# A 16-image approximate-matmul convolution block: ranking lookups, first-map scatters, second-layer centring and next-image loads at other steps

## The chip, the cores and the metric

The kernel runs on one core of one Trainium2 chip. A core has five engines that run their own instruction queues: TensorE (PE in the profile; its weight loads are PEld), VectorE (DVE), ScalarE (ACT), GpSimd (POOL) and SyncE (SP, whose queue issues most DMAs). 16 DMA engines serve all queues. The metric is the device time of one execution in microseconds (us); lower is better.

## The reference

A block of 16 images (256 channels, 28 x 28), all in fp32. Each image is group-normalized (32 groups), then goes through two layers in which a 3x3 convolution is replaced by a lookup: per channel, the 9-element patch is compared with 16 centroids, the softmax of the negated distances weighs the centroids, and the weighted centroid goes through the weights.

```python
def amm_conv3x3(x, centroids, w_sub):          # C channels, k=16 codes, s=9
    p = patches3x3(x)                          # b, n, C, s
    d = sum(p*p) - 2*einsum('bncs,cks->bnck', p, centroids) + sum(centroids*centroids)
    attn = softmax(-d)                         # over the 16 codes
    lut = einsum('cks,cso->cko', centroids, w_sub)
    return einsum('bnck,cko->bno', attn, lut)

out = relu(bn1(amm_conv3x3(gn(x), centroids1, wsub1)))
out = bn2(amm_conv3x3(out, centroids2, wsub2))
out = out * sigmoid(relu(mean(out) @ w1 + b1) @ w2 + b2)
result = x + relu(out + gn(x))
```

## The kernel before

**Tiling and steps.** The work is cut into blocks: layer (2) x image (16) x half of the channels (`hh`) x half of the rows (`t`), 128 blocks in all, four to an image. A block takes two steps, so an image is 8 steps; layer 0 of image `b` starts its blocks at step `8b`, layer 1 follows from step 128. In each step PE runs, in this order: 32 records of logits (`lg`, L388), 64 records of either denominators (`nb`, L452, in even steps) or numerators (`na`, L438, in odd steps), 32 more logits, and then a product of up to 18 records (`acc`, L522). The four blocks of an image are combined with seven products instead of eight (a Strassen scheme), for which POOL forms differences of the quotients (`mix`, L529 and L531). Products of steps 8n+6 and 8n+7 have 14 and 4 records, so these two steps are short.

**What one block needs.** SP loads 3x3 patches from a padded image in DRAM (`home1`, `home2`) into `pt` (L373, L376), six DMAs for each step. PE makes logits, ACT the exponentials (L399), PE `nb`, ACT and DVE the reciprocal (L462, L466, L480), DVE spreads it (L495), PE makes `na`, and DVE (L514) or ACT and POOL (L508, L503) scale it to the quotients `qp` and `qo`.

**Side work.** Between the blocks of layer 0 the kernel prepares layer 1. Channels are sorted by a score after image 0 (the *ranking*): `rank_row` loads the scores of all channels (L643, L644), `rank_make` compares them on POOL (L651 to L654), `rank_sum` counts on DVE (L659), `rank_look` gathers a table row for each channel (L666, two indirect DMAs on POOL), and `rank_cols` copies its columns (L675). From image 1 on, `to_home2` scatters the first layer's output to DRAM in that order (L594, four indirect DMAs for each image). Image 0 was finished before the order was known, so its two maps are kept in `d_h0`, read back by `h0_load` (L691) and scattered by `h0_put` (L594 again, with the source `st`). Later steps build layer 1's codes in the same staging tile `st`: `prep_wd2` and `prep_wd3` add the squared norms (L285, L290, L291), `prep_wd4` centres them over the 16 codes (`center_mean`: a DVE sum L295 and a scaling L296, then two POOL subtractions L297 and L743), `prep_keep` writes them out (L746); `prep_cw0` and `prep_cwa` (L751, L761) and `prep_cwb` (L769 to L771) build the other two. `load_x` (L162) reads the next image into the single tile `xt`; `gn_stats` and `gn_apply` read it.

**What sets the order.** Nothing is reordered by a scheduler here. Each piece of work is entered with `at(step, place, function, ...)`, and all entries are emitted in the order of `(step, place)`; each engine runs its instructions in that order, waiting on semaphores where data or buffers are not ready. Within a step, logits stand at 0.1 and 1.1, `nb` and `na` at 1.0, patch loads at 1.5, products at 2.0.

```python
def at(cl, sub, f, *a, **kw):
    jobs.setdefault((cl, sub), []).append((f, a, kw))
...
at(g + 5, 2.5, mix, us[0], mm, us[1], us[0])
at(g + 7, 1.35 if mm in (4, 0) else 1.25, mix, us[1], mm, us[2], us[1])
```

Of the kernel before, what the change touches and what calls it, by code (L numbers as in the profile page):

```python
# [12 lines left out]
ALU = mybir.AluOpType  # L13
AX = mybir.AxisListType
# [3 lines left out]
P = 128  # L18
# [7 lines left out]
K = 16  # L26
# [49 lines left out]
def kernel(  # L76
# [20 lines left out]
    nc = tc.nc  # L97
# [180 lines left out]
    cst = const.tile([P, 64], F32, name="cst")  # L278
# [9 lines left out]
    def center_add(wf, c0, w, sq, step=None):  # L288
        ps = small_bank("sqp", step)
        nc.tensor.matmul(ps[:, :w], lhsT=nhalf_sb, rhs=sq[:, :w], start=True, stop=True)  # L290
        nc.vector.tensor_add(wf[:, c0 : c0 + w], wf[:, c0 : c0 + w], ps[:, :w])  # L291

    def center_mean(wf, n, eng=None):
        g = wf.rearrange("p (g k) -> p g k", k=K)
        nc.vector.tensor_reduce(cst[:, : n // K], g, axis=AX.X, op=ALU.add)  # L295
        nc.vector.tensor_scalar_mul(cst[:, : n // K], cst[:, : n // K], 1.0 / K)  # L296
        (eng or nc.vector).tensor_sub(g, g, cst[:, : n // K].unsqueeze(2).to_broadcast([P, n // K, K]))  # L297

    def center(wf, n):
        for c0 in range(0, n, 256):  # L300
            center_add(wf, c0, 256, center_sq(wf, c0, 256))
        center_mean(wf, n)
# [381 lines left out]
    pw = {}  # L684
# [51 lines left out]
    def prep_wd3(part, step):  # L736
        center_add(pw["st"][:, 512:1536], 384 * part, min(384, 1024 - 384 * part), pw["sq"], step)

    def prep_wd4():
        st = pw["st"]  # L740
        center_mean(st[:, 512:1536], 1024, nc.gpsimd)
        f = st[:, 512:1536].rearrange("p (g n) -> p g n", n=32)
        nc.gpsimd.tensor_sub(f, f, kbias.unsqueeze(1).to_broadcast([P, 32, 32]))  # L743

# [151 lines left out]
    def at(cl, sub, f, *a, **kw):  # L896
        jobs.setdefault((cl, sub), []).append((f, a, kw))
# [10 lines left out]
    for j, u in enumerate(blocks):  # L908
        gi, g = 8 * (j // 4), 2 * j
# [11 lines left out]
    for j, u in enumerate(blocks):  # L921
        g = 2 * j
# [35 lines left out]
    for l in range(2):  # L958
        for b in range(B):
            n = l * B + b  # L960
            g = 8 * n
            us = blocks[4 * n : 4 * n + 4]
            for c, w, r, ks in PRODUCTS:
                at(g + c, 2.0, product, (n, c), us[r], w, ks, step=g + c)
            for mm in (1, 2, 3, 4, 0):
                at(g + 5, 2.5, mix, us[0], mm, us[1], us[0])
                at(g + 7, 1.35 if mm in (4, 0) else 1.25, mix, us[1], mm, us[2], us[1])
                at(g + 8, 1.37 if mm == 1 else 1.4, mix, us[0], mm, us[2], us[0])
                at(g + 10, 1.4, mix, us[0], mm, us[0], us[3])
            c11, c12, c21, c22 = (0, 0), (0, 1), (1, 0), (1, 1)  # L970
            at(g + 6, 0.0, acc_copy, l, b, c11, (n, 5))
            at(g + 6, 2.02, acc_copy, l, b, None, (n, 6))
            at(g + 8, 0.0, acc_add, l, b, None, (n, 7))
            at(g + 8, 2.02, acc_add, l, b, c21, (n, 8), c11)
            at(g + 10, 0.0, acc_add, l, b, c22, (n, 9), c11, pop=False)
            at(g + 10, 0.01, acc_add, l, b, c21, (n, 9))
            at(g + 10, 0.05, reg_add, l, b, c12, c22, None)
            at(g + 10, 0.06, reg_add, l, b, c22, c21, None)
            at(g + 10, 2.02, acc_add, l, b, c12, (n, 10))
            at(g + 12, 0.0, acc_add, l, b, c11, (n, 11))  # L980
            at(g + 12, 2.02, acc_add, l, b, c21, (n, 12), op=ALU.subtract)
            if l == 0 or b == B - 1:
                at(g + 11, 1.9, norm_out, l, b, *c12)
                at(g + 11, 1.91, norm_out, l, b, *c22)
                at(g + 12, 1.9 if l else 0.05, norm_out, l, b, *c11)
                at(g + 13, 1.06, norm_out, l, b, *c21)
            else:
                for o in range(NB):
                    at(g + 12 + o, 1.9, norm_both, b, o)
            if l == 0:  # L990
                for o in range(2):
                    if b == 0:
                        at(g + 13, 1.9, rank_score, o)
                        at(g + 13, 1.91, rank_keep, o)
                        at(g + 12 + 2 * o, 0.65 if o else 1.93, h0_keep, o)
                    else:
                        for r in range(2):
                            at(g + 12 + o + (o and r), (0.06, 1.97)[r] if o == 0 else (1.805, 2.9)[r], to_home2, b, o, r)
                if b + 1 < B:
                    at(*((g - 2, 2.6) if b else (1, 1.65)), load_x, b + 1)  # L1000
                    for q in range(NB):
                        at(*((g, 0.3) if b else (3, 1.9)), gn_stats, b + 1, q)
                    at(*((g + 1, 2.1) if b else (4, 1.02)), gn_mean, b + 1, step=g + 1 if b else 4)
                    at(*((g + 3, 2.1) if b else (4, 1.11)), gn_var, b + 1, step=g + 3 if b else 4)
                    for q in range(NB):
                        at(g + 4, 1.9, gn_apply, b + 1, q)
                        at(g + 4, 1.92, to_home1, b + 1, q)
            else:
                last = b == B - 1
                at(*((g + 11, 0.6) if last else (g + 13, 2.6)), load_x, b, last)  # L1010
                at(g + 14 - last, 2.1, se_hidden, b, g + 14 - last)
                at(*((g + 14, 1.05, se_gate, b, g + 14) if last else (g + 17, 2.1, se_gate, b, g + 17)))
                at(*((g + 14, 1.05) if last else (g + 18, 0.3)), se_recip, b)
                for q in range(NB):
                    at(*((g + 12, 0.4) if last else (g + 19, 1.9)), finish_norm, b, q)
                    if not last:
                        at(g + 18, 1.9, finish_gate, b, q)
                        at(g + 20, 0.05, finish_sum, b, q)
                        at(g + 20, 1.9, finish_relu, b, q)
                        at(g + 20, 2.2, finish_add, b, q)  # L1020
                        at(g + 20, 2.25, store, b, q)
                    else:
                        at(g + 14, 1.92, finish_fast, b, q)
                        at(g + 14, 1.92, store, b, q)
                if b == B - 1:
                    at(g + 11, 1.9, flags)
                    at(g + 12, 2.9, flag_sum)
# [13 lines left out]
    for o in range(2):  # L1041
        at(14, 2.95, rank_make, o)
        at(16, 0.2, rank_sum, o)
        at(18, 2.15, rank_look, o)
    for o in range(2):
        at(19 + o, 2.7, rank_cols, o)
        at(24 + 2 * o, 0.6 + 2 * o, h0_load, o)
        for r in range(2):
            at(25 + 2 * o + r, 0.2 if r else 1.9, h0_put, o, r)
        at(32 + 2 * o, 2.6, codes_load, o)  # L1050
        for i in range(2):
            at(33 + 2 * o, 1.9, codes_put, o, i)
        for part in range(2):
            c = 40 + 8 * o + 2 * part
            at(c, 2.6, sub_load, o, part)
            at(c + 1, 1.9, sub_put, o, part)
# [3 lines left out]
    for part in range(3):  # L1060
        c = (68, 70, 76)[part]
        at(c, 1.95, prep_wd2, part)
        at(c + 1, 2.1, prep_wd3, part, c + 1)
    at(78, 1.9, prep_wd4)
    at(78, 2.7, prep_keep, d_wd[1])
    at(80, 2.6, prep_cw0)
    at(82, 1.9, prep_cwa)
    for part in range(4):
        at((83, 84, 91, 92)[part], (2.3, 1.5, 2.3, 1.5)[part], prep_cwb, part)
    at(92, 2.7, prep_keep, d_cwb)  # L1070
    at(92, 2.3, load_se)
    for n in range(3):
# [3 lines left out]
    g = 8 * B  # L1076
# [195 lines left out]
```

## Time and profile before

| What | us |
|---|---|
| Median of 3 runs | 2642.16 |
| Lowest and highest of them | 2637.82 and 2643.82 |
| The profiled execution: its time | 2646.4 |
| The profiled execution: its span, first to last instruction | 2644.9 |
| Mean granted PE clock in it | 0.996 |

| Engine | Busy us | Share of the span |
|---|---|---|
| PE | 2595.2 | 98% |
| POOL | 1905.0 | 72% |
| DVE | 1758.2 | 66% |
| ACT | 1357.2 | 51% |

The page of the profile gives busy time for each engine and the chain of work that ended last, followed back from the last instruction. A timeline gives for one engine the start, the length, the line, the operation, what it writes and reads, and in brackets the idle time ahead of it with what ended it. Matmuls overlap and their ends are modelled, so a stall of PE often shows as a longer group rather than as idle time: 32 logits take 0.94 us in most steps, 64 `na` or `nb` records 2.92 us. A quiet image of layer 0 (steps 98 to 106) takes 80.03 us from its first `nb` to the next image's, and each image of layer 1 takes 80.32.

### The profile page before, as it was taken

How to read it: one execution, taken by the hardware profiler on the slowest of the kernel's cores; microseconds unless marked ns; L12 is line 12 of the kernel's file. 1: busy time of each engine (PE TensorE's matmuls, PEld its weight loads, DVE VectorE, ACT ScalarE, POOL GpSimd, SP SyncE). 2: the span in 40 equal slices, each digit the busy share in tenths (PEclk: the TensorE clock that was granted, in tenths of full speed). 3: DMA queues.
4: the chain of work that ended last, by engine and by line, in shares of the span. 5: the costliest groups of instructions: out<-in, count | busy, mean ns of one | idle time of the engine just before them, and what ended most of it. 6: DMA issues, size and time to landing. Idle time of an engine off the chain costs nothing.

```text
span 2644.9 us, 85672 instructions
## 1 busy us (share of the span) xinstructions
PE 2595.2 (98%) x36984; PEld 1266.4 (48%) x36984; DVE 1758.2 (66%) x3760; ACT 1357.2 (51%) x1874; POOL 1905.0 (72%) x1330
## 2 busy tenths in 40 slices
PE   5999999999999999999999999999999999999997
PEld 2444444444444445444444444444444444444444
DVE  4776566665566655665666776767677667767665
ACT  4444444454444544444454555556555655555653
POOL 3866667765667666676567878778878787777786
PEclk9999999999999999999999999999999999999999
DMA  8656656666556666665664445544454544445441
GB/s 201 163 158 173 175 163 167 186 181 168 143 133 157 172 170 165 173 167 148 159 176 109 105 120 128 125 117 107 111 128 121 121 116 115 114 118 127 114 118 48
DMA packets 217735, 374.37 MB, mean 142 GB/s; under 512 B 30136, under 2 KB 187624, under 8 KB 217352
## 3 DMA queue, kind: packets, MB, share of 16 engines
q1 hardware_dynamic: 210408, 334.87, 50.8%
q0 software_dynamic: 6944, 33.95, 3.6%
q8 instruction: 295, 4.83, 0.8%
q14 instruction: 88, 0.72, 0.1%
HBM read 288.93 MB, written 79.80 MB: 139 GB/s over the span
## 4 chain that ended last, share of the span: by engine, by line
PE 96%; DVE 2%; POOL 1%; DMA 0%; issue 0%; ACT 0%; DVEq 0%; POOLq 0%
PE acc L522 51%; PE lg L388 17%; PE nb L452 14%; PE na L438 13%; POOL qp L531 0%; DVE rb L495 0%; DMA pt<-home 0%; DVE r L480 0%; PE sqp L290 0%; DVE qp L514 0%; PE sep L820 0%; POOL qp L503 0%; PE sep L809 0%; DMA xt<-in_x 0%; PE gnp L341 0%
## 5 line engine op out<-in xcount | busy, mean ns | idle before, releaser
L399 ACT ACTIVATE e<-lg 128x784 f32<-128x784 f32 x960 | 738.5, 820 | 661.7 <-PE lg L388 657.2
L531 POOL TENSOR_TENSOR qp<-qp,qp 128x784 f32<-128x784 f32 x512 | 943.5, 1867 | 156.1 <-DVE qp L514 155.6
L522 PE MATMUL acc<-qp,w_S 128*128 128x392 f32 x2048 | 734.5, 501 | 2.5 <-POOL qp L531 1.1
L495 DVE STREAM_SHUFFLE rb<-r 128x392 f32<-128x392 f32 x1024 | 551.0, 604 | 0.0
L522 PE MATMUL acc<-qp,w_A 128*128 128x392 f32 x1536 | 546.5, 499 | 0.0
L522 PEld LDWEIGHTS acc<-qp,w_S 128*128 128x128 f32 x2048 | 376.1, 190 | 346.5 <-issue 51.6
L388 PE MATMUL lg<-pt,wd 32*32 32x392 f32 x16384 | 492.8, 504 | 18.5 <-DMA pt<-home 5.2
L522 PEld LDWEIGHTS acc<-qp,w_A 128*128 128x128 f32 x1536 | 284.1, 190 | 247.6 <-DVE qp L514 39.6
L466 DVE SCALAR_TENSOR_TENSOR r<-nb,kst,r 128x392 f32<-128x392 f32 x128 | 79.9, 624 | 461.2 <-ACT r L462 449.0
L438 PE MATMUL na<-e,cwa 64*32 64x392 f32 x8192 | 376.5, 492 | 1.2 <-ACT e L399 0.7
L452 PE MATMUL nb<-e,cwb 64*32 64x392 f32 x8192 | 376.8, 494 | 0.1
L514 DVE TENSOR_TENSOR qp<-na,rb 128x784 f32<-128x784 f32 x352 | 333.6, 972 | 60.2 <-PE na L438 46.4
L503 POOL TENSOR_TENSOR qo<-qo,rb 128x392 f32<-128x392 f32 x128 | 131.2, 1025 | 315.6 <-DVE rb L491 314.8
L480 DVE RECIPROCAL r<-r 128x392 f32<-128x392 f32 x128 | 333.2, 2603 | 4.4
L503 POOL TENSOR_TENSOR qp<-qp,rb 128x784 f32<-128x784 f32 x160 | 297.0, 1866 | 3.4 <-issue 0.3
L452 PEld LDWEIGHTS nb<-e,cwb 64*32 64x32 f32 x8192 | 191.3, 107 | 178.4 <-issue 28.6
L438 PEld LDWEIGHTS na<-e,cwa 64*32 64x32 f32 x8192 | 182.7, 106 | 186.0 <-issue 75.8
L388 PEld LDWEIGHTS lg<-pt,wd 32*32 32x32 f32 x16384 | 122.7, 103 | 299.5 <-issue 249.2
L462 ACT ACTIVATE r<-nb,kst 128x392 f32<-128x392 f32 x128 | 86.7, 677 | 169.0 <-PE nb L452 169.0
L423 POOL TENSOR_TENSOR z<-z,mx 128x1568 f32<-128x1568 f32 x32 | 91.8, 2869 | 94.7 <-DVE mx L417 94.7
L508 ACT COPY qp<-na 128x784 f32<-128x784 f32 x160 | 129.9, 812 | 24.6 <-PE na L438 23.0
L529 POOL TENSOR_TENSOR qo<-qo,qo 128x392 f32<-128x392 f32 x128 | 131.2, 1025 | 0.0
(151 smaller groups left out, 1658.1 us busy)
## 6 DMA issues: line engine op xcount, KB each, us to landing
pt<-home SPq DMA_DIRECT2D x768, 209.0 KB
pt<-home SPq DMA_DIRECT2D x756, 104.5 KB
home<-xpad SPq DMA_DIRECT2D x31, 899.0 KB
xt<-in_x SPq DMA_DIRECT2D x30, 784.0 KB
out_dram<-y SPq DMA_DIRECT2D x32, 392.0 KB
d_wS<-st SPq DMA_DIRECT2D x12, 192.0 KB
w_S<-d_wS SPq DMA_DIRECT2D x4, 576.0 KB
w_A<-in_ws SPq DMA_DIRECT2D x3, 576.0 KB
```

What stands on the lines that cost most here:

```text
L388: nc.tensor.matmul(bk[32 * c : 32 * c + 32, :N].rearrange("p (r w) -> p r w", w=W), lhsT=wts["wd", u["hh"]][32 * i : 32 * i + 32, mm, c, : ...
L399: nc.scalar.activation(eg[:, 2 * i : 2 * i + 2, :], bk[:, :, :N], AF.Exp, scale=2.0)
L438: nc.tensor.matmul(bs[32 * i : 32 * i + 32, r, :N], lhsT=wts["cwa", u["hh"]][64 * r : 64 * r + 64, mm, i, :], rhs=es[64 * r : 64 * r + 64, ...
L452: nc.tensor.matmul(bs[32 * i : 32 * i + 32, r, :N], lhsT=wts["cwb", u["hh"]][64 * r : 64 * r + 64, mm, i, :], rhs=es[64 * r : 64 * r + 64, ...
L480: nc.vector.reciprocal(u["r"], u["r"])
L495: nc.vector.stream_shuffle(rb[:, r, :], u["r"], mask_of(2 * mm + r))
L503: nc.gpsimd.tensor_tensor(q, q, u.pop(("rb", mm)), ALU.mult)
L508: nc.scalar.copy(pair(u, mm), u.pop(("na", mm))[:, :, :N])
L514: nc.vector.tensor_mul(pair(u, mm), u.pop(("na", mm))[:, :, :N], rb)
L522: nc.tensor.matmul(accs[key][:, :N], lhsT=wl[w][:, k, :], rhs=us["q", k], start=first and n == 0, stop=last and n == len(ks) - 1,)
L529: nc.gpsimd.tensor_tensor(out_u["q", 8], in0["q", 8], in1["q", 8], ALU.subtract)
L531: nc.gpsimd.tensor_tensor(pair(out_u, mm), pair(in0, mm), pair(in1, mm), ALU.subtract)
```

## The change

Only the places in the order change, and `center_mean` is cut in two functions so that its DVE part can stand at a place of its own. `load_x` of the images after the second moves one step ahead. The computation is the same.

```diff
-    def center_mean(wf, n, eng=None):
+    def center_sum(wf, n):
+        nc.vector.tensor_reduce(cst[:, : n // K], wf.rearrange("p (g k) -> p g k", k=K), axis=AX.X, op=ALU.add)
+        nc.vector.tensor_scalar_mul(cst[:, : n // K], cst[:, : n // K], 1.0 / K)
+
+    def center_mean(wf, n):
+        center_sum(wf, n)
         g = wf.rearrange("p (g k) -> p g k", k=K)
...
+        nc.vector.tensor_sub(g, g, cst[:, : n // K].unsqueeze(2).to_broadcast([P, n // K, K]))
...
+    def prep_wd_sum():
+        center_sum(pw["st"][:, 512:1536], 1024)
+
     def prep_wd4():
         st = pw["st"]
-        center_mean(st[:, 512:1536], 1024, nc.gpsimd)
+        g = st[:, 512:1536].rearrange("p (g k) -> p g k", k=K)
+        nc.gpsimd.tensor_sub(g, g, cst.unsqueeze(2).to_broadcast([P, 64, K]))
         f = st[:, 512:1536].rearrange("p (g n) -> p g n", n=32)
         nc.gpsimd.tensor_sub(f, f, kbias.unsqueeze(1).to_broadcast([P, 32, 32]))
...
-                    at(*((g - 2, 2.6) if b else (1, 1.65)), load_x, b + 1)
+                    at(*((g - 3, 2.6) if b else (1, 1.65)), load_x, b + 1)
...
-        at(18, 2.15, rank_look, o)
+        at(17, 1.9, rank_look, o)
     for o in range(2):
-        at(19 + o, 2.7, rank_cols, o)
-        at(24 + 2 * o, 0.6 + 2 * o, h0_load, o)
+        at(18, 2.7, rank_cols, o)
+        at(24 + 4 * o, 0.1 if o else 0.6, h0_load, o)
         for r in range(2):
-            at(25 + 2 * o + r, 0.2 if r else 1.9, h0_put, o, r)
+            at(*((25, 1.9), (27, 1.9), (28, 1.96), (30, 1.85))[2 * o + r], h0_put, o, r)
...
-    at(78, 1.9, prep_wd4)
+    at(77, 2.2, prep_wd_sum)
+    at(78, 0.5, prep_wd4)
...
-    at(82, 1.9, prep_cwa)
+    at(83, 1.9, prep_cwa)
     for part in range(4):
-        at((83, 84, 91, 92)[part], (2.3, 1.5, 2.3, 1.5)[part], prep_cwb, part)
+        at((84, 84, 91, 92)[part], (0.5, 1.5, 2.3, 1.5)[part], prep_cwb, part)
```

## The prediction

> **What bounds the kernel now.** The page comes first: busy times, and the chain that ended last.
>
> ```profile
> PE 2595.2 (98%) x36984; PEld 1266.4 (48%) x36984; DVE 1758.2 (66%) x3760; ACT 1357.2 (51%) x1874; POOL 1905.0 (72%) x1330
> PE 96%; DVE 2%; POOL 1%; DMA 0%; issue 0%; ACT 0%; DVEq 0%; POOLq 0%
> ```
>
> PE sets the end, and no matmul is removed, so the change can win only what PE loses in stalls at the places it touches. I take a stall as a group's length over its usual one (0.94 for 32 lg, 2.92 for 64 na), or as the distance between two groups over that in the quiet image of steps 98 to 106.
>
> Second, the piece of the chain of waits around step 79 (start, length, what).
>
> ```profile
> 815.30 1.11 DVE cst L295
> ...
> 816.71 1.95 POOL st L297
> 818.73 2.38 POOL st L743
> ...
> 822.26 5.51 POOL qp L531 x3
> ...
> 830.54 0.96 POOL qo L529
> 831.50 1.81 POOL qp L531
> 833.31 0.04 issue
> 833.35 2.98 PE acc L522 x4
> ```
>
> Here PE is not the bound: the codes' sum on DVE, two subtractions on POOL, then POOL's differences, for which the product of step 80 waits. From the na at 815.27 to the na at 837.22 are 21.95 us; the quiet image has 16.83 between the same two (1062.02 to 1078.85). Lost: 5.12.
>
> Third, the timelines of PE and POOL at the ranking and the first map's scatters.
>
> ```profile
> 204.28 0.94 PE L388 MATMUL lg<-pt,wd 32*32 32x392 f32 x32
> 205.15 5.03 PE L438 MATMUL na<-e,cwa 64*32 64x392 f32 x64
> ```
> ```profile
> 205.23 1.12 POOL L666 DMA_INDIRECT idx<-in_ids,ri  x1 [0.17 <-issue]
> 206.65 0.97 POOL L666 DMA_INDIRECT idx<-in_ids,ri  x1 [0.30 <-issue]
> ```
> ```profile
> 301.86 0.97 POOL L594 DMA_INDIRECT home<-st,col  x1 [0.30 <-issue]
> ```
> ```profile
> 302.03 2.17 PE L388 MATMUL lg<-pt,wd 32*32 32x392 f32 x32
> ```
>
> The na group waits for nothing named and still takes 2.11 too long while POOL issues two gathers; the lg group at 302.03 takes 1.23 too long behind a scatter 0.17 earlier. The same pattern: scatter at 220.25, lg at 220.94 +0.58; scatter at 279.72, lg at 280.00 +0.48. An indirect DMA issued while PE is in acc costs nothing: the pair of `codes_put` at 355.95 and 357.26 lies in the acc of 351.78 to 358, and the lg at 358.02 takes 0.94. So an indirect DMA's price is read from PE's group at its issue: 0 in acc, 0.5 to 1.2 at the start of lg, 2.1 for a pair in na. Why is not shown; only when.
>
> **The parts.** *Centring (5.12 now).* The DVE sum (1.22) and scaling (0.20) go behind the addition of step 77, into this gap:
>
> ```profile
> 805.11 0.42 DVE L291 TENSOR_TENSOR st<-st,sqp 128x256 f32<-128x256 f32 x1 [4.64 <-PE sqp L290]
> 809.56 0.63 DVE L466 SCALAR_TENSOR_TENSOR r<-nb,kst,r 128x392 f32<-128x392 f32 x1 [4.03 <-ACT r L462]
> ```
>
> 805.53 + 1.42 = 806.95, 2.6 before DVE's next work; without that cover 1.42 would go to the reciprocal. POOL is idle from 811.98 to 816.71 (4.73) and the subtractions take 1.94 + 2.38 = 4.32 plus 0.1, so they end at 816.4. SP's write of the codes waits until then, not 821.1; behind it on SP stand only step 79's patch loads, due at about 819. Step 81's stay behind the eight loads of `prep_cw0` (9.66 us of issue), some 5 us ahead of their use. The scatter of 821.25 follows the subtractions on POOL, so it falls at 816.5, in the na of 815.27. Nearest rows: scatters 1.28 into an nb with lg 1.57 later (702.85, 1032.48) cost 0; 0.85 into it (1273.12) 0.16; the one at 821.25 with nb 0.66 later 0.53. I take 0.3 of 0 to 0.6. Gain 4.8.
>
> *Other codes (0.67 now).* Four DVE products (2.24) at 857.42 hold up the addition at 859.59 that na waits for (858.82 to 862.34 instead of 2.85). Behind step 83's spreads DVE is idle 4.38 in the quiet image (1026 to 1030.42): covered. `prep_cwb` goes behind the scatter into POOL's idle 6.7 before 885.91; its 5.4 us (twelve operations, 871.56 to 878) fit as now. Gain 0.67.
>
> *Ranking (2.11 + 0.58 now).* The gathers go behind step 17's scaling, which ends at 191.93; the first falls into acc (187.3 to 193.1), the second, 1.42 later, onto lg and nb. Bounds 0 (`codes_put`) and 1.2 (largest lg stall); I take 0.5, as for most single ones. POOL's next work starts at 194.83, after both. The fourteen copies (1.77) go to 205.2, where POOL is then idle until 212; the scatter at 220.25 comes 0.9 earlier, at the phase that costs 0 to 0.16: 0.1. Gain 2.1.
>
> *First map (0.48 + 1.23 now).* The scatter of 279.72 goes to step 27's place, used already at 296.18 inside acc at no cost. Its staging tile is then free at about 300, so SP waits from 296 to 300 for the second load, with nothing but patch loads due at 303 behind it; the load took 6 us beside patches (285.16 to 291), so the third scatter falls at 304 to 306 in acc (303 to 309): 0. The image's own scatter behind it moves from 304.05 to 306, still in acc. The fourth goes to 328.48 and pushes the next one to 329.8, at the end of a 14-record acc: 0 to 1.2, 0.2 taken (the pair at 355.95 is nearest). Gain 1.5.
>
> *Next-image loads (2.20 now).* In the short steps 8n+6 and 8n+7, groups are longer beside the load: lg at 576.98 (+0.51), 735.89 (+0.23), 743.17 (+0.60), 1147.29 (+0.28), acc to lg at 985.12 (+0.58). One step ahead the steps are 10.7 us, and the patch loads of the next step follow 6 us later. But only some loads show a stall, and 1226.08 has one (0.94) with no load near. The first moved load, of step 5, only goes ahead of weights issued at 74.24 and needed in step 11, near 129. I take 0.7 left, of 0 to 2.2. Gain 1.5.
>
> *What the load pushes back.* For image 3 it now stands at step 13, on SP ahead of the write of image 0's second map and of the scores' row:
>
> ```profile
> 159.53 0.33 SPq L643 DMA_DIRECT2D row<-d_sc  x1
> ```
> ```profile
> 162.98 0.94 POOL L651 TENSOR_SCALAR row<-row,score 128x256 f32<-128x256 f32 x1 [0.23 <-issue]
> 169.76 5.53 POOL L531 TENSOR_TENSOR qp<-qp,qp 128x784 f32<-128x784 f32 x3
> 179.00 7.33 POOL L531 TENSOR_TENSOR qp<-qp,qp 128x784 f32<-128x784 f32 x4
> ```
> ```profile
> 181.32 1.48 PE L522 MATMUL acc<-qp,w_S 128*128 128x392 f32 x4
> ```
>
> The row's packets ran from 160.50 to 162.47, POOL starts on them at 162.98 and is then never idle until 191.93. The first of the four L531 ends at 180.83; PE needs it at 181.32, so about 0.4 is spare. The image's 256 packets of 3136 bytes took 4.6 beside patch loads (166.5 to 171.1); 16 for each DMA engine at 131 ns are 2.1. With little else moving at 158 I take the 2.1: POOL starts at 164.9, 1.9 late, and PE stalls 1.5 in step 16 (0.6 to 4.2).
>
> After the idle of step 80 the granted clock is 0.50 for 3.4 us (833.20 to 836.60), behind a stretch of 3.40 us in which PE was busy 1.50. A stall of 1.9 in 3.4 was enough here; 1.5 lies just under it, and what the half clock cost is read from the acc records there: about 1.5. The Trainium skill (TensorE: Matmul & The Clock Gate, Part 1) puts the half clock behind at least one idle window of about 3.4 us. By that rule a 1.5 us stall never costs clock; by this row one of 1.9 does, and the sum would be 1.5 higher. The trace does not agree that the whole window must be idle.
>
> **Sum.** 4.8 + 0.67 + 2.1 + 1.5 + 1.5 - 1.5 = 9.1 us. The profiled execution took 2646.4 (span 2644.9 and 1.5 around it), so 2637.3 on its scale. It lies 4.2 over the median of the runs, which I take for all of its parts alike: 2642.16 - 9.1 = 2633.0.
>
> **Rivals.**
> *The scores' row comes much later.* If the load takes its 4.6, POOL is 4.6 late, PE stalls 4.2, and the half clock adds 1.5: 4.2 lost beyond the forecast, 2637.2. For: POOL's unbroken run to 191.93. Against: at 158 to 160.5 the map's write has the DMA engines almost alone.
>
> *The stalls only move.* Gathers, scatters and loads find PE in dense groups again at the old prices (2.69 + 1.71 + 2.20 = 6.6 instead of 1.5 left), and only centring and codes win: 9.1 - 5.1 = 4.0, so 2638.2. For: it is not shown why PE slows. Against: the pair at 355.95, in the very place where the gathers go.
>
> *Slower: the load starves PE in every image.* Behind the start-up thirteen loads now meet the scatter of place 1.805 and two rounds of patch loads in steps 8n+5 and 8n+6. At the largest lg stall, 1.23 each, that is 16.0; with the other parts' gain (9.1 - 1.5) it gives 2650.6. It makes the kernel slower from 0.6 us per image. Against: packets thin out at the end of step 8n+5 (1054 to 1057 in the quiet image); PE has an 18-record acc there.
>
> *It doesn't do what it says.* Each engine waits where data is missing, so a moved piece could simply wait at its new place. Gathers, sum and scatters have their inputs by then; only the third scatter waits, in idle POOL time.
>
> **How the numbers follow.** Forecast 0.60, late row 0.16, stalls that move 0.16, slower 0.08. The time is the forecast's, 2633.0. Its own bounds are 2642.2 - 12.4 = 2629.8 (nothing left of the 12.4 lost now) and, with every residue at its upper end (0.6 + 1.2 + 0.16 + 1.2 + 2.2 + 4.2 = 9.6), 2639.4. The three runs spread by 6, so 2628 below; 2640 above takes in both middle rivals and leaves out the slow one and a little. A change of 0.2% (5.3 us) is about what a measurement of this kernel tells from none: faster than 2636.9 holds most of the forecast (0.56) and under half of each middle rival (0.14 together): 0.70. Slower 0.08, the rest 0.22.
>
> **What would show it.** The na near 205 at 2.92 and the lg near 302 at 0.94; no full PE idle near 830 and no half clock there; the DVE sum near 805.5; POOL's L651 later than 162.98 and a longer acc near 181. I am wrong if the images of layer 0 from the fourth on take more than 80.2 each, or if step 16 loses over 4.

## The result and the profile after

| | before | after |
|---|---|---|
| Median of 20 runs each, us | 2640.84 | 2643.35 |
| Lowest and highest | 2636.38 and 2644.90 | 2640.16 and 2649.48 |
| Profiled execution: time, span | 2646.4, 2644.9 | 2642.01, 2640.5 |

The ratio is 1.0013 (95% interval 1.0007 to 1.0019): no change by the bound of 0.2%, if anything slower by 2 to 5 us, where 9.1 us had been forecast as a gain. The two profiled executions say the opposite (4.4 faster). That of before took more than any of its 20 runs, that of after less than its median.

The page of after, busy time and the chain that ended last:

```profile
PE 2588.7 (98%) x36984; PEld 1264.4 (48%) x36984; DVE 1763.8 (67%) x3760; ACT 1357.5 (51%) x1874; POOL 1905.3 (72%) x1330
PE 96%; DVE 2%; POOL 1%; DMA 1%; issue 0%; ACT 0%; SPq 0%; DVEq 0%; POOLq 0%
```

PE still sets the end. Beside before, DMA's share of the chain is 1% in place of 0%, SP's queue appears with 0%, and DVE has 5.6 us more busy time (1758.2 before).

What was to go is gone. PE's timeline of after at the ranking and the first map (start, length, operation):

```profile
195.70 2.92 PE L455 MATMUL nb<-e,cwb 64*32 64x392 f32 x64
...
206.42 2.92 PE L441 MATMUL na<-e,cwa 64*32 64x392 f32 x64
...
300.12 0.94 PE L391 MATMUL lg<-pt,wd 32*32 32x392 f32 x32
```

These groups have their usual lengths; before, the na took 5.03 and the lg at 302.03 2.17. Two new losses stand against that. The first is at step 78. DVE and POOL there:

```profile
801.38 1.22 DVE L294 TENSOR_REDUCE cst<-st 128x64 f32<-128x1024 f32 x1
802.63 5.20 DVE L295 TENSOR_SCALAR cst<-cst 128x64 f32<-128x64 f32 x1
807.75 0.61 DVE L469 SCALAR_TENSOR_TENSOR r<-nb,kst,r 128x392 f32<-128x392 f32 x1
```
```profile
799.47 5.54 POOL L534 TENSOR_TENSOR qp<-qp,qp 128x784 f32<-128x784 f32 x3
804.98 1.01 POOL L532 TENSOR_TENSOR qo<-qo,qo 128x392 f32<-128x392 f32 x1
805.95 1.83 POOL L534 TENSOR_TENSOR qp<-qp,qp 128x784 f32<-128x784 f32 x1
807.91 1.93 POOL L748 TENSOR_TENSOR st<-st,cst 128x1024 f32<-128x1024 f32 x1
```

The scaling takes 5.20. In the profile of before, where POOL was idle beside it, it took 0.20:

```profile
816.44 0.20 DVE L296 TENSOR_SCALAR cst<-cst 128x64 f32<-128x64 f32 x1
```

In after it starts in the second of five operations on SBUF that follow each other on POOL without a gap, and ends when POOL stops. L469, which starts 3.69 behind the start of the nb where nothing holds it (scale_pool, below), starts 6.07 behind it here (nb at 801.68), and PE pays:

```profile
811.56 0.95 PE L391 MATMUL lg<-pt,wd 32*32 32x392 f32 x32 [1.28 <-issue]
...
818.78 2.92 PE L455 MATMUL nb<-e,cwb 64*32 64x392 f32 x64
```

The second, and larger, comes behind the image load that is now issued in step 93. SP's queue and PE there:

```profile
957.86 0.35 SPq L753 DMA_DIRECT2D d_cwb<-st  x1
961.07 0.61 SPq L376 DMA_DIRECT2D pt<-home  x1
...
964.22 0.58 SPq L379 DMA_DIRECT2D pt<-home  x1
964.90 0.39 SPq L162 DMA_DIRECT2D xt<-in_x  x1
967.32 0.55 SPq L376 DMA_DIRECT2D pt<-home  x1
```
```profile
976.68 1.58 PE L525 MATMUL acc<-qp,w_S 128*128 128x392 f32 x4
981.73 0.95 PE L391 MATMUL lg<-pt,wd 32*32 32x392 f32 x32 [3.47 <-DMA pt<-home]
982.61 4.59 PE L455 MATMUL nb<-e,cwb 64*32 64x392 f32 x64
```

Step 93's patch loads start at 961.07, and behind them goes the image's load of 784 KB. The next patches, those of step 94, follow it by 2.4 us. Patches are loaded two steps ahead, so these are for step 96, and PE waits 3.47 for them at the first lg of that step. (Some expectations below name this lg after step 94, and the same one behind the load of step 5, the first lg of step 8, after step 7.) Then the granted clock is 0.50 from 983.28 to 986.69, which lengthens the nb from 2.92 to 4.59.

A last, small one was forecast: the first map's write and the image's load stand ahead of the scores' row, POOL starts on the row late, and a product of step 16 waits.

```profile
164.53 0.94 POOL L654 TENSOR_SCALAR row<-row,score 128x256 f32<-128x256 f32 x1 [1.36 <-issue]
```
```profile
182.49 1.58 PE L525 MATMUL acc<-qp,w_S 128*128 128x392 f32 x4 [0.56 <-POOL qp L534]
```

### The profile page after: what moved, and what is told of

Same layout as the page of the kernel before. It is cut to its first block, busy times and chain, and to the rows that moved or that the text cites. A ratio compares the mean times of both kernels' runs of the same rounds, so it can differ in the third digit from the quotient of the medians.

```text
span 2640.5 us, 85671 instructions
## 1 busy us (share of the span) xinstructions
PE 2588.7 (98%) x36984; PEld 1264.4 (48%) x36984; DVE 1763.8 (67%) x3760; ACT 1357.5 (51%) x1874; POOL 1905.3 (72%) x1330
## 4 chain that ended last, share of the span: by engine, by line
PE 96%; DVE 2%; POOL 1%; DMA 1%; issue 0%; ACT 0%; SPq 0%; DVEq 0%; POOLq 0%
PE acc L525 51%; PE lg L391 17%; PE nb L455 14%; PE na L441 13%; POOL qp L534 0%; DMA pt<-home 0%; DVE rb L498 0%; PE sqp L290 0%; DVE qp L517 0%; DVE r L483 0%; PE sep L827 0%; POOL qp L506 0%; PE sep L816 0%; DMA xt<-in_x 0%; DMA d_sc<-score_t 0%
## 5 line engine op out<-in xcount | busy, mean ns | idle before, releaser
L498 DVE STREAM_SHUFFLE rb<-r 128x392 f32<-128x392 f32 x1024 | 550.6, 604 | 0.0
L469 DVE SCALAR_TENSOR_TENSOR r<-nb,kst,r 128x392 f32<-128x392 f32 x128 | 80.1, 626 | 465.9 <-ACT r L465 453.6
L483 DVE RECIPROCAL r<-r 128x392 f32<-128x392 f32 x128 | 333.2, 2603 | 4.4
```

What stands on the lines that cost most here:

```text
L483: nc.vector.reciprocal(u["r"], u["r"])
L498: nc.vector.stream_shuffle(rb[:, r, :], u["r"], mask_of(2 * mm + r))
```

## The experiments

Three theories were set against each other. "Load": the moved image loads give the gain back. "Lock": the held scaling does. "Base": the profiled execution of before was not a usual one, so there was less to win.

The readings rest on the length of each image of layer 0 in one profile, from the nb of step 8n+2 to that of step 8n+10 (80.02 when quiet). Image 1 holds steps 10 to 18, image 2 the ranking, image 3 most of the first map's scatters, image 9 the centring, image 10 the other codes, image 11 steps 90 to 98.

| kernel | 1 | 2 | 3 | 6 | 9 | 10 | 11 | ratio to before (95%) |
|---|---|---|---|---|---|---|---|---|
| before | 80.04 | 82.72 | 81.74 | 80.67 | 85.64 | 80.75 | 80.79 | |
| before_again | 80.03 | 82.27 | 81.51 | 80.67 | 85.73 | 80.75 | 80.73 | |
| after | 80.85 | 80.02 | 80.02 | 80.02 | 82.05 | 80.02 | 85.50 | 1.0013 (1.0007 to 1.0019) |
| after_again | 82.07 | 80.74 | 80.86 | 80.03 | 82.53 | 80.02 | 85.58 | 1.0008 (0.9999 to 1.0017) |
| load_only | 80.70 | 82.72 | 81.88 | 80.02 | 84.09 | 80.76 | 85.17 | 1.0024 (1.0013 to 1.0034) |
| centre_only | 80.03 | 82.75 | 81.57 | 80.71 | 82.54 | 80.18 | 80.26 | 0.9992 (0.9983 to 1.0001) |
| rank_scatter_only | 80.27 | 80.76 | 80.27 | 80.87 | 84.11 | 80.74 | 80.75 | 0.9989 (0.9980 to 0.9998) |
| loads_back | 80.42 | 80.73 | 81.48 | 80.92 | 82.43 | 80.02 | 80.10 | 0.9978 (0.9969 to 0.9987) |
| load12_back | 80.92 | 80.75 | 81.07 | 80.02 | 82.43 | 80.02 | 80.11 | 0.9994 (0.9985 to 1.0003) |
| load1_moved | 80.13 | 80.71 | 80.19 | 80.56 | 82.49 | 80.02 | 80.61 | 0.9980 (0.9971 to 0.9989) |
| load93_moved | 80.03 | 80.03 | 80.03 | 80.09 | 82.07 | 80.03 | 85.50 | 1.0007 (0.9998 to 1.0016) |
| sp_cleared | 81.09 | 80.02 | 80.02 | 80.02 | 82.02 | 80.02 | 80.02 | 0.9995 (0.9986 to 1.0004) |
| scale_stt | 80.90 | 80.77 | 80.71 | 80.02 | 82.48 | 80.02 | 86.51 | 1.0015 (1.0006 to 1.0024) |
| scale_psum | 80.32 | 80.78 | 80.26 | 80.51 | 82.31 | 80.02 | 80.79 | 0.9982 (0.9973 to 0.9991) |
| scale_pool | 80.03 | 80.59 | 80.84 | 80.74 | 80.97 | 80.48 | 80.25 | 0.9973 (0.9962 to 0.9984) |
| mixed_pool | 80.17 | 80.72 | 81.16 | 80.02 | 81.00 | 80.16 | 80.57 | 0.9972 (0.9963 to 0.9981) |
| cleared_pool | 80.17 | 80.03 | 81.18 | 80.04 | 80.46 | 80.03 | 80.03 | 0.9970 (0.9959 to 0.9982) |

The runs were taken in four groups, each beside the kernel before and each on another chip: before_again, loads_back, load12_back and scale_stt; load_only, centre_only, rank_scatter_only and scale_psum; after_again, load1_moved, scale_pool and mixed_pool; load93_moved, sp_cleared and cleared_pool. The kernel before took 2644.8 to 2645.4 us in the first three groups and 2640.6 in the last, so only ratios go from group to group; 0.0010 is 2.6 us.

**Was the first profile usual?** The kernel before, unchanged (before_again).

> The kernel before, unchanged, profiled a second time. Theory 'base' (the profiled execution of before was not a usual one; part of its loss at steps 78 to 80 belongs to that execution): the distance from the na of step 79 to the nb of step 80 is 2 us or more under the 15.31 of the first profile, with no half clock near 833, and the span is near 2640. Theory 'load' and theory 'lock' (the loss at centring was real and what was won there was given back elsewhere in the changed kernel): 15.3 again, a half clock near 833, span near 2644.

The distance that the expectation means, 15.31 in the first profile, runs from the nb of step 80 to the na of step 81. It is 15.43 here, with a half clock from 831.52 to 834.94: "base" falls in this form, though the span, 2641.5, lies nearer to its 2640 than to its rivals' 2644. But load_only and rank_scatter_only hold the same code at steps 78 to 80 and take 13.82, with image 9 at 84.1. The view by windows (PE's busy time, then those of the other engines, granted clock, DMA share, GB/s), before and then load_only:

```profile
829.50:833.00 3.50, 1.80 (x5) 0.49 (x3) 2.40 (x9) 0.00 (x0) 3.50 (x3) 1.00 0.76 180
833.00:836.50 3.50, 3.15 (x20) 1.42 (x36) 0.13 (x1) 0.00 (x0) 3.50 (x3) 0.52 0.73 107
```
```profile
829.50:833.00 3.50, 2.63 (x8) 1.16 (x7) 3.50 (x8) 0.70 (x2) 3.50 (x3) 1.00 0.81 169
833.00:836.50 3.50, 2.34 (x6) 0.97 (x6) 0.66 (x3) 0.00 (x0) 3.50 (x3) 1.00 0.76 140
```

PE waits the same two times in load_only:

```profile
833.29 0.93 PE L522 MATMUL acc<-qo,w_S 128*128 128x392 f32 x2 [1.16 <-POOL qo L529]
835.09 1.58 PE L522 MATMUL acc<-qp,w_S 128*128 128x392 f32 x4 [0.87 <-POOL qp L531]
```

1.16 and 0.87 here, 1.18 and 0.87 in before, but no half clock follows. So 1.5 of the 5.1 us that stood in the profile as the centring's loss is there in some profiles only. The last section shows what separates them.

**The loads.** All back, or only the one of step 93 back:

```diff
-                    at(*((g - 3, 2.6) if b else (1, 1.65)), load_x, b + 1)
+                    at(*((g - 2, 2.6) if b else (1, 1.65)), load_x, b + 1)                        # loads_back
+                    at(*((g - 2 if b == 12 else g - 3, 2.6) if b else (1, 1.65)), load_x, b + 1)  # load12_back
```

> The changed kernel with every image load back one step later, where it stood before. Theory 'load': image 11 falls from 85.50 to about 80.8 us, the acc of step 16 loses its 0.83 and step 7 its 0.67, while images 6 and 13 get 0.65 and 0.28 back; together 5.3 less than the changed kernel, so about 2638. Theory 'lock' or theory 'base': image 11's loss stays or goes with no effect on the median, and the time stays within 1.5 of 2643.

> The changed kernel with one load alone, the one issued in step 93, back at step 94. Theory 'load' in its narrow form (only the load behind SP's late queue of step 92 costs): image 11 falls from 85.50 to about 80.8, everything else stays, so 4.7 less than the changed kernel, about 2638.7. In its wide form (the moved load costs in all images in executions that the profile does not show): about 2641 or more. Theories 'lock' and 'base': within 1.5 of 2643.

Measured 0.9978 and 0.9994; the changed kernel has 1.0008 to 1.0013. With all loads back it is faster than before, by 5.8 us. Image 11 falls to 80.1 in both, as "load" had it. As ratios, the expected times are 0.9993 for loads_back and 0.9995 for load12_back: the second is met, the first is missed by some 4 us to the good. In this one group load12_back takes 3.8 us more than loads_back, so other moved loads cost something too. Then the loads alone, in the kernel before (the opposite edit):

> The kernel before with nothing changed but the loads' step (8n+5 in place of 8n+6). Theory 'load', wide: it alone takes about what separates the changed kernel (ratio 1.0013) from the one with all loads back (0.9978), so it is some 9 us slower than before, ratio 1.0034; image 11 about 85.5 long and stalls behind step 5. Narrow (only step 93): 4.5 slower, 1.0017. As the prediction had it: 1.5 faster from groups no longer beside a load, 1.5 lost in step 16: no change.

6.3 us slower (3.4 to 9.0), between the narrow form and the wide one, with both ratios inside the interval (1.0013 to 1.0034): the moved loads are what turned the gain round, and "no change", which the prediction had made of them, is outside the interval. Which of them? One was moved at a time, with all others back (b == 1, or b == 12, in place of the condition above):

> The changed kernel with all loads back but one, the one issued in step 5 while the kernel still starts up. With the load of step 93 alone back the ratio was 0.9994, with all back 0.9978. Theory 'step 5' (this load gives the rest): about 0.9992, 3.5 slower than all back, and a wait for patches at the lg of step 7 in some profiles. Rival: the rest came from step 13 and many small ones; then 0.9978 to 0.9981.

> The changed kernel with all loads back but the one of step 93. Theory 'step 93' (this load is nearly all of the loss): image 11 near 85.5 again and 4.7 to 5.2 slower than all loads back (0.9978), ratio 0.9996 to 0.9998. Theory 'steps 5 and 13 too' (they are half of it): 0.9988 or less.

The load of step 5 alone costs nothing that its median shows (0.9980 against 0.9978), so that theory falls. Step 93's load alone makes the kernel as slow as before (1.0007), more than expected, with the expected 0.9996 to 0.9998 at the edge of the interval, and image 11 is 85.50 again. Step 5's load is not harmless in every execution, though. PE's first lg of step 8 in load12_back and in after_again:

```profile
92.82 1.79 PE L391 MATMUL lg<-pt,wd 32*32 32x392 f32 x32 [3.28 <-DMA pt<-home]
```
```profile
93.71 1.12 PE L391 MATMUL lg<-pt,wd 32*32 32x392 f32 x32 [2.81 <-DMA pt<-home]
```

The other five profiles with that load moved lose under 1.1 us there; loads_back, with it at its old place, loses 0.77. The load of step 13 was not moved alone. That the loads of steps 5 and 13 together cost some 4 us is read from two differences within a group, each good to some 3 us: load12_back over loads_back (3.8, with the eleven other loads in it, which cost nothing in mixed_pool below), and sp_cleared over cleared_pool below (6.1, of which the scaling's place takes about 1.5). How these 4 us divide stays open.

Why step 93? The load stayed where the change puts it, and SP's step 92 was cleared of two other things:

```diff
-    at(92, 2.7, prep_keep, d_cwb)
-    at(92, 2.3, load_se)
+    at(94, 2.7, prep_keep, d_cwb)
+    at(100, 2.3, load_se)
```

> The changed kernel, all loads where the change puts them, with two other things taken out of SP's step 92: the gate's weights go to step 100 and the write of the other codes to step 94. Theory 'late queue': step 93's patches go out as early as in a quiet image (some 6 us ahead of the lg of step 94, not 1.4), the load behind them, the next patches 7 us after it; image 11 falls from 85.5 to 80.5 or less and the kernel is some 5 faster than the changed one (1.0008 to 1.0013), about 0.9991. Rival (the 784 KB beside patches cost it wherever SP stands): image 11 stays above 83 and the ratio above 1.0000.

SP's queue and PE in sp_cleared:

```profile
956.66 0.59 SPq L376 DMA_DIRECT2D pt<-home  x1
...
960.01 0.58 SPq L379 DMA_DIRECT2D pt<-home  x1
960.69 0.39 SPq L162 DMA_DIRECT2D xt<-in_x  x1
967.38 0.55 SPq L376 DMA_DIRECT2D pt<-home  x1
```
```profile
976.50 1.58 PE L525 MATMUL acc<-qp,w_S 128*128 128x392 f32 x4
978.01 0.94 PE L391 MATMUL lg<-pt,wd 32*32 32x392 f32 x32
```

Step 93's patches start 4.4 earlier and the load 4.2, the next patches start 6.7 behind the load, PE waits for nothing and image 11 is quiet. The same 784 KB at the same step cost nothing when SP is on time. Which of the two things made SP late, the gate's weights or the write, was not tried apart. The ratio, 0.9995, is 3.4 to 4.7 us under the changed kernel's two; about 5 had been expected.

**The centring.** Alone in the kernel before, with the other codes:

> The kernel before with the centring and the other codes' pieces moved as in the change, nothing else. The prediction's two terms: 4.8 + 0.67 = 5.5 faster, ratio 0.9979. Theory 'lock' (the scaling held 5.2 us beside POOL gives 1.5 back): image 9 about 82.0 and image 10 about 80.0 in place of 85.64 and 80.75, so 4.3 faster, 0.9984. Theory 'base' (the loss at step 80 is not there in a usual execution): under 2 us faster, 0.9993 or more.

2.1 us faster (4.5 faster to 0.3 slower): the prediction's 5.5 is outside, "lock" (4.3) and "base" (under 2) both fit. Beside the two profiles of the same group that keep the old centring (84.1), image 9 gains 1.6; image 10 gains 0.6. Why the scaling is held was tried in two ways. First with another DVE instruction, in the changed kernel:

```diff
-        nc.vector.tensor_scalar_mul(cst[:, : n // K], cst[:, : n // K], 1.0 / K)
+        nc.vector.scalar_tensor_tensor(cst[:, : n // K], cst[:, : n // K], 1.0 / K - 1.0, cst[:, : n // K], op0=ALU.mult, op1=ALU.add)
```

> The changed kernel with the scaling of the codes' sums written as another DVE instruction at the same place (each sum times -15/16, plus the sum, in place of times 1/16). Theory 'lock' (the scaling took 5.20 us because a POOL operation ran beside that kind of DVE instruction, not because of data): it takes 0.2 to 0.4 us and ends near 803, the products of step 78 lose the 1.28 behind them, and the kernel is 1.4 faster than the changed one, about 2642. If it is data, a semaphore or DVE's queue that held it, it ends near 807.8 as before and the time stays at 2643.4.

```profile
804.78 5.21 DVE L295 SCALAR_TENSOR_TENSOR cst<-cst 128x64 f32<-128x64 f32 x1
```

5.21 beside POOL, and no gain in time (1.0015): a miss for "lock" as it was put there. Between these two instructions, which both read SBUF, the kind doesn't decide. Then with the sums in PSUM, and all loads back:

```diff
-        center_sum(pw["st"][:, 512:1536], 1024)
+        ps = pw["ps"][:, 256:320]
+        nc.vector.tensor_reduce(ps, pw["st"][:, 512:1536].rearrange("p (g k) -> p g k", k=K), axis=AX.X, op=ALU.add)
+        nc.vector.tensor_scalar_mul(cst, ps, 1.0 / K)
```

> The changed kernel with all loads back, and with the sums of the codes written to PSUM, from where the same DVE scaling reads them. Theory 'lock' (a DVE instruction with its inputs in SBUF is held while a POOL operation runs; the first try kept two inputs there): the scaling takes 0.2 to 0.3 us while POOL's L534 runs, DVE's L469 starts as soon as the nb is done, and the step from 77 to 78 falls by 1.3; 1.4 faster than with the loads back alone (ratio 0.9978), so 0.9973, about 6.8 under before. If data or a semaphore holds it, it takes 5.2 us again and the ratio stays at 0.9978.

DVE, POOL and PE in scale_psum:

```profile
803.30 0.22 DVE L746 TENSOR_SCALAR cst<-sqp 128x64 f32<-128x64 f32 x1
```
```profile
800.06 5.50 POOL L535 TENSOR_TENSOR qp<-qp,qp 128x784 f32<-128x784 f32 x3
```
```profile
803.58 2.87 PE L456 MATMUL nb<-e,cwb 64*32 64x392 f32 x64 [1.23 <-DVE cst L746]
```

The same DVE instruction at the same place, behind the same sum, takes 0.22 in the middle of POOL's L535 when its input is in PSUM. So neither data nor a semaphore held it: its reading from SBUF while POOL worked did. That doesn't go for every DVE instruction on SBUF. In after the 128 reciprocals (L483) take 2.59 to 2.61 us and the 1024 shuffles (L498) 0.58 to 0.64, each with its input in SBUF, and 62 of the first and 577 of the second have POOL at work beside them for over 95% of their length. The Trainium skill (SBUF — State Buffer, Who interferes with whom) says that GpSimd shares its one pair of SBUF ports with VectorE's second pair, and that a `tensor_scalar` in a two-port mode, or a VectorE instruction with two SBUF inputs against a GpSimd operation that reads SBUF, takes that pair for its whole length; the later one waits. It exempts `tensor_reduce`. The runs agree in all four forms: 5.20, 5.21, 0.22 from PSUM, and 1.22 for the sum. The mode itself stands in no trace, and the wait was longer than one POOL instruction: it lasted through the rest of one and three more. The time didn't fall clear of the noise (0.9982 against 0.9978, intervals overlapping). In the profile the nb waits 1.23 for the scaling, because the bank of PSUM stays taken longer: a new wait in the place of the old.

Last, the scaling on POOL, in front of its subtractions, with all loads back:

```diff
-        center_sum(pw["st"][:, 512:1536], 1024)
+        nc.vector.tensor_reduce(cst, pw["st"][:, 512:1536].rearrange("p (g k) -> p g k", k=K), axis=AX.X, op=ALU.add)
...
         st = pw["st"]
+        nc.gpsimd.tensor_scalar_mul(cst, cst, 1.0 / K)
```

> The changed kernel with all loads back and the scaling of the codes' sums done by POOL, in front of its two subtractions, where it can't be held by POOL and holds nothing on DVE. Theory 'lock': DVE's L469 of step 78 starts as soon as the nb is done, nothing else waits, image 9 falls from 2.4 to about 0.9 over the quiet image; 1.5 faster than all loads back (0.9978), so 0.9972. Rival: POOL's three operations end later and the scatter behind them or the product of step 80 takes the gain; 0.9978.

```profile
805.63 0.38 POOL L747 TENSOR_SCALAR cst<-cst 128x64 f32<-128x64 f32 x1
```

It costs POOL 0.38, image 9 falls to 80.97 as expected, and the ratio is 0.9973 against the expected 0.9972. What it wins is read from image 9: 1.5 less than in loads_back (82.43), and as much less than in load1_moved of its own group (82.49). The medians alone (0.9978 and 0.9973, intervals overlapping) could not show it.

**Ranking and first map**, alone in the kernel before:

> The kernel before with the ranking's and the first map's pieces moved as in the change, nothing else. The prediction's two terms: 2.1 + 1.5 = 3.6 faster, ratio 0.9986; the nb of step 18 and the na of step 31 at 2.92 to 3.1. Theory 'stalls move' (the indirect DMAs meet dense groups again): about 0.55 in the nb of step 18 and 0.7 to 0.9 in the na of step 31, as in the profile with all loads back, and 1.5 to 2.3 faster, 0.9992.

2.9 us faster (0.5 to 5.3), between the prediction's 3.6 and the rival's 1.5 to 2.3, and the interval holds both. The nb of step 18 is 0.52 too long, as the rival had it, the na of step 31 only 0.24, and images 2 and 3 together gain 3.4 over before.

**The changed kernel once more, and versions drawn from all this.**

> The changed kernel once more, beside the others of this call. If the parts simply add, the three single parts give -3.1 (rank and first map), -1.3 to -2.1 (centring and codes) and +6.3 (loads), so +1 to +2 against before, ratio 1.0004 to 1.0013. If the parts disturb each other (the second theory of why all gains were lost), it is more than 5 slower, 1.002 or more. In the profile: the idle before the lg of step 94 near 3.5 us and image 11 near 85.5 again.

1.0008, so 2.1 slower: the parts add up within their intervals (-2.1 - 2.9 + 6.3 = +1.3), and nothing shows that they disturb each other. mixed_pool is scale_pool with the loads moved but for steps 5, 13 and 93; cleared_pool has step 93's moved too, with SP cleared as above.

> As the last, but only the loads issued in steps 5, 13 and 93 are back; the others stand where the change puts them, where images 6, 7 and 13 lost 0.65, 0.5 and 0.3 to loads in short steps before. Theory 'load' (only SP's crowded places make the moved load dear): 1.3 faster than the last, ratio 0.9967, the best of all. Rival (a moved load costs a little everywhere): no faster than the last, 0.9972 or more.

> The last, with the scaling on POOL and the loads of steps 5 and 13 back. If the three mend different losses, it is as fast as the kernel with those two loads and step 93's back (0.9972) or a little better, 0.9970. If the moved weights or the moved write find a new collision, over 0.9980.

0.9972 and 0.9970, as mixed_pool's rival and cleared_pool's theory had it. They beat both kernels: cleared_pool by 7.9 us against before (4.8 to 10.8). That the moved loads win anything of their own isn't shown (0.9972 beside scale_pool's 0.9973).

## Why the prediction was wrong, point by point

**Bound and base.** PE is the bound, and the stalls read from the page were there. The 4.2 us by which the profiled execution lay above the median were taken "for all of its parts alike"; what the profiles show is that some stalls come in some executions and not in others, the half clock behind the centring among them.

**Next-image loads: the step that failed.** The prediction costed them at a gain of 1.5 and, through the scores' row, a loss of 1.5. Measured: 6.3 lost. That is the largest part of what separates the forecast gain of 9.1 from the result; the centring with the other codes gave 3.4 less than forecast, the ranking with the first map 0.7 less. The sentence that failed is "One step ahead the steps are 10.7 us, and the patch loads of the next step follow 6 us later". It was read from the quiet image. At step 93 SP is late, and they follow 2.4 us later. The profile of before shows it, in SP's queue at a step that the prediction left out:

```profile
966.43 0.43 SPq L233 DMA_DIRECT2D b_sb<-in_se_b  x1
967.75 0.35 SPq L746 DMA_DIRECT2D d_cwb<-st  x1
969.52 0.60 SPq L373 DMA_DIRECT2D pt<-home  x1
...
975.83 0.54 SPq L373 DMA_DIRECT2D pt<-home  x1
```

Step 93's patches start 1.4 ahead of the lg at 970.96, against 5.8 in the quiet image of after (1042.11 and 1047.95). Before, the time behind them was free. The forecast went through steps 5 and 13, where the load passes other work, but not through each of the places where it lands. Its slower rival named the load, in every image; it was mainly one. The load of step 5 had been given no cost. With that of step 13 it takes some 4 us in two of the groups, and the wait at step 8 stands in two of the seven profiles with it moved. The gain of 1.5 from groups no longer beside a load showed in no median.

**The scores' row.** Mechanism right: POOL starts on the row 1.55 later than before (1.9 was forecast), and 0.83 is lost in step 16 where 1.5 was forecast (image 1 is 0.68 to 2.05 over a quiet one in the other profiles with that load moved). The rival of a much later row was not needed.

**Centring.** 4.8 forecast, some 1.6 measured. The DVE sum and scaling were said to fit into a gap of DVE. The sum did; the scaling did not, because POOL worked in that gap: 1.5 to 1.6 given back, which POOL's scaling returns (image 9 from 82.43 to 80.97). Another 1.5 was the half clock, absent from the profiles of the group in which this was measured. POOL's half of the reasoning held: the subtractions end at 812.28 in after (at 821.1 in before), and PE no longer waits near step 80.

**Other codes.** 0.67 forecast, 0.6 to 0.7 in image 10. Right.

**Ranking and first map.** 3.6 forecast, 2.9 (0.5 to 5.3) measured. Right as far as the interval tells, with the residues inside their bounds.

## What to carry to other kernels

A move that is repeated in a loop must be checked at every iteration that has other work in its queue, not in the quiet one: one of fourteen loads cost more than the 1.5 us that all of them were to win. A gap of VectorE is not free for every instruction while GpSimd works in it: the scaling on SBUF took 5.20 us for 0.20, but 0.22 when it read PSUM, and reductions, reciprocals and shuffles kept their lengths. On the engine that consumes its result it cost 0.38. And a kernel's single profile can show a stall that other executions don't have: a second profile of before, or one with an unrelated edit, tells which.

## What the runs showed of the hardware

The half clock. Up to the last 15 us of a profile, the stretches of 0.50 in the records are 3.41 us long, or 6.83. In each profile all changes of the clock lie on one grid of 3.41 us, which stands differently from profile to profile. Two waits of 1.16 and 0.87, 0.9 apart, gave no half clock in load_only, and 1.18 and 0.87 gave one in before. On the grid they differ: in before both waits, but for the last 0.18 us, fall into one window, which ends with the change of the clock at 833.17; in load_only a boundary, at 834.39, cuts the second wait. The two windows (before, then load_only; PE's busy time comes first):

```profile
829.75:833.17 3.42, 1.55 (x4) 0.30 (x2) 2.15 (x9) 0.00 (x0) 3.42 (x3) 1.00 0.78 174
```
```profile
830.98:834.39 3.41, 2.07 (x6) 0.68 (x4) 2.67 (x10) 0.00 (x0) 3.41 (x3) 1.00 0.77 167
```

The other profiles agree. Of the grid's windows at full clock, from 30 us to the last 15 of all 17 profiles, 34 are followed by a half clock; PE was busy in them for 0 to 1.73 us. Every window with less than 1.41 is among them, none with more than 1.73, and between these both occur. So the same waits cost 1.5 us or nothing by where the grid stands. The Trainium skill (TensorE: Matmul & The Clock Gate, Part 1) describes a window of 3413 ns that runs freely and isn't reset when a kernel starts; the records agree. The Trainium skill's rule there that the half clock comes after at least one idle window is not borne out if it means a whole window without work: in before PE was busy for 1.55 us of it.

The indirect DMAs' price changes with the runs. The second gather of the ranking starts 0.64 ahead of the nb of step 18 in both after and loads_back, and the nb takes 2.92 in the first and this in the second:

```profile
194.26 3.45 PE L455 MATMUL nb<-e,cwb 64*32 64x392 f32 x64
```

In every profile with the early gathers from the three groups in which before took 2644.8 to 2645.4, image 2 is 80.59 or more; in after, beside which before took 2640.8, and in the last group it is 80.02 or 80.03. What differs there stays open.
